# A two-layer float32 kernel: block sums stored from GpSimd's queue, one weight item prepared later, squares taken one by one

## The chip, the core and the metric

One Trainium2 chip, one of its cores. The metric is the device time of one execution in microseconds. Engines are named as in the profile: PE (TensorE, with PEld for its weight loads), DVE (VectorE), ACT (ScalarE), POOL (GpSimd), SP (SyncE). All data is float32.

## What is computed

Input x is 4 x 1024 x 32 x 32: four batches, 1024 channels, 1024 positions ("tokens"). Layer 0 is attention with 16 heads of 64, layer 1 is a bottleneck of convolutions with batch norms.

```
# layer 0, per batch, tokens x channels
q, k, v = x @ w_qkv.T + b                    # each 1024 x 1024
q, k    = rope(q), rope(k)                   # rotate even/odd pairs by cos, sin
q, k    = rmsnorm(q), rmsnorm(k)             # over all 1024 channels
ctx     = softmax(q k' / 8) v                # per head
x       = rmsnorm(ctx @ w_proj.T) * w + x
# layer 1
h = relu(bn(conv1x1(x, w1)));  h = relu(bn(conv3x3(h, w2)));  h = bn(conv1x1(h, w3))
out = relu(x + softplus(scale) * h)
```

## The kernel before

**Products.** The four projections (q, k, v and the output projection, called y) are 1024 x 1024 matrix products computed with seven block products in place of eight (Winograd's form of Strassen's scheme). That needs sums of weight blocks, called S1 to S4, and sums of blocks of x. In batch 0 the projections of q and k use one level of the scheme (`project`); each group g of weight blocks has its sums made by `operands` (L224): four loads on SP's queue (L221), four VectorE instructions (L231 to L234), and four stores of the sums to HBM, to the tensor `wd`, issued from ScalarE's queue (L239), each 256 KB. Everything else uses two levels (`project2`), and reads sums that were made ahead and stored: `wd` holds the sums of the first level, `wd2` those of the second.

**Weight items.** An item is the preparing of one outer block k (0 to 6) of one weight matrix for the second level (`prepare`, L384: four loads, VectorE L391 to L394, four stores to `wd2` from GpSimd's queue, L396), or of one block of first-level sums (`prepare_blocks`, L400: loads L405, sums L408 to L411, stores L413). In batch 0 the items of WV and the first of WQ are spread over the q, k and v projections by `weight_parts` (L1049), with their loads on GpSimd's queue, into tiles that are otherwise free (`unused`, later `rq`, the room of v, and a tile of `ts`). The other items (of WP, the rest of WQ, and WK) are made in the attention of batch 0: a list `todo` (L1127), loaded on SP's queue, and made one or two per pair of heads (L799).

**Order.** The order of TensorE, GpSimd, VectorE and ScalarE instructions is that in which the program records them. SP's queue holds the other loads. A planner spaces work: `product_done(share)` (L256) is called after each matrix product and advances a clock, 1 per product of one level and 0.5 per product of two levels; `after(n, step)` (L253) runs a step n later; `waiting` holds longer steps that run when there is room. `product_done` runs steps that are due in the order in which they were given.

**Buffers.** Weight blocks go through a ring of eight buffers of 256 KB (`chunk`, tag "w"). A load into a buffer waits for the matmuls and for the store that read the buffer before. One group of `operands` takes five of the eight, so that the last load of a group waits for the store of the first sum of the group before it.

**Rotary step.** When q (and k) of a batch are complete, `inverse_rms` (L661) sums squares by a matmul against ones (L670), and `rope` (L686) turns the eight blocks one by one: VectorE makes `qs` and `q` (L700), and GpSimd adds `qs` to `q` by two accumulating DMAs (L704). The buffers of `qs` are three, so a block waits for the additions of the third before it.

**Squares.** The sum of squares is gathered block by block. In `project2`, when a 512 x 512 block of the result is finished, `ready` (L600) plans for each of its four pieces a `done`: for k a bias on ScalarE (L608), then the square on ScalarE (L585 or L588); VectorE adds it half a unit later (L592). The pieces 0 and 1 are planned 0.5 later, the pieces 2 and 3 one unit later, beside the copies out of PSUM that ScalarE makes for TensorE (L516, L537, L542, L551, L565).

**Attention** (L744) works on pairs of heads: 16 score matmuls (L761), exponentials on ScalarE (L768), sums of the probabilities on VectorE (L772, L774), 16 matmuls with v (L780), for eight pairs and two halves of the queries. The program ends with the convolutions. A second copy of the program, with a shifted softmax, follows under a condition that is not met here.

Of the kernel before, what the change touches and what calls it, by code (L numbers as in the profile page):

```python
# [34 lines left out]
WQ, WK, WV, WP, W1 = 0, NFB, 2 * NFB, 3 * NFB, 4 * NFB  # L35
# [38 lines left out]
@with_exitstack  # L74
def layers_kernel(ctx, tc, x, wblk, w2, w3, vecs, cos, sin, out):
    nc = tc.nc
    flag = ctx.enter_context(tc.tile_pool(name="flag", bufs=1))
    bad = flag.tile([1, 1], mybir.dt.int32, name="bad")
    program(tc, x, wblk, w2, w3, vecs, cos, sin, out, bad)
    shifted = nc.values_load(bad[0:1, 0:1], min_val=0, max_val=P)  # L80
    with tc.If(shifted > 0):
        program(tc, x, wblk, w2, w3, vecs, cos, sin, out, None)
# [3 lines left out]
def program(ctx, tc, x, wblk, w2, w3, vecs, cos, sin, out, bad):  # L86


    nc = tc.nc
# [21 lines left out]
    def col(name, i=0):  # L111
        return vec[:, COL[name] + i : COL[name] + i + 1]
# [32 lines left out]
    wd = dram.tile([4 * NG, len(SUMS), P, NH * P], F32, name=f"wd{u}")  # L145
# [7 lines left out]
    with tc.tile_pool(name=f"st{u}", bufs=2) as st, ExitStack() as s:  # L153
# [48 lines left out]
        def temp(name):  # L202
            return tmp.tile([P, CH], F32, tag="tmp", name=name)
# [8 lines left out]
        def chunk(name):  # L212
            return wring.tile([P, NH, P], F32, tag="w", name=name)

        def flat(t):
            return t.rearrange("p a b -> p (a b)")

        def block(base, f, ih, name):

            t = chunk(f"w_{name}")  # L220
            nc.sync.dma_start(flat(t), wblk[base + f][:, ih * NH * P : (ih + 1) * NH * P])  # L221
            return t

        def operands(base, g, name):  # L224


            at = base // NT * NG + g
            a11, a12 = (block(base, g, ih, f"{name}_1{ih}") for ih in range(2))
            a21, a22 = (block(base, g + NG, ih, f"{name}_2{ih}") for ih in range(2))
            s1 = chunk(f"w_{name}_s1")  # L230
            nc.vector.tensor_tensor(s1, a21, a22, ALU.add)  # L231
            nc.vector.tensor_tensor(a21, a11, a21, ALU.subtract)
            nc.vector.tensor_tensor(a11, s1, a11, ALU.subtract)
            nc.vector.tensor_tensor(a12, a12, a11, ALU.subtract)  # L234
            spend(4 * TT)

            def keep():
                for o, t in enumerate((a11, s1, a21, a12)):
                    nc.scalar.dma_start(wd[at, o], flat(t))  # L239

            after(1, keep)
            return [a11, s1, a21, a12, a22]


# [2 lines left out]
        later, waiting = [], deque()  # L247
        pace = {"at": 0, "room": 0.0, "hold": False, "tables": 0.0}

        def spend(cost):  # L250
            pace["room"] -= cost

        def after(n, step):  # L253
            later.append((pace["at"] + n, step))

        def product_done(share=1.0):  # L256
            pace["at"] += share
            pace["room"] = min(pace["room"] + share, 1.2)
            due = [s for at, s in later if at <= pace["at"]]
            later[:] = [(at, s) for at, s in later if at > pace["at"]]  # L260
            for step in due:
                step()
            while waiting and pace["room"] > 0 and not pace["hold"]:
                next_waiting()

        def next_waiting():
            cost, step = waiting.popleft()
            spend(cost)
            step()

        def rest(leave=0):
            while later or len(waiting) > leave:
                product_done()
# [15 lines left out]
        def project(b, base, bs, ts, outs, bias, squares, tag, w1=None):  # L289
# [40 lines left out]
            for g in range(NG):  # L330
                c11 = outs(g)[0]
                o2 = bank("o2", f"pb_{tag}_{b}_{g}")
                product(o2, w1[NG + g], "A12", True, True)
                after(1, lambda o2=o2, c11=c11, g=g: add(c11, o2, g))
                after(2, lambda c11=c11: squares(c11, 0))
                product_done()
                if g == 1:
                    w2[0] = operands(base, 0, f"{tag}_{b}_0b")
# [45 lines left out]
        def prepare(which, base, k, alloc, queue):  # L384

            a11, a12, a21, a22 = a = alloc(f"pre_{which}_{k}")
            for i, t in enumerate(a):
                quarter(t, base, k, i // 2, i % 2, queue)

            def make():  # L390
                nc.vector.tensor_tensor(a22, a21, a22, ALU.add)  # L391
                nc.vector.tensor_tensor(a21, a11, a21, ALU.subtract)
                nc.vector.tensor_tensor(a11, a22, a11, ALU.subtract)
                nc.vector.tensor_tensor(a12, a12, a11, ALU.subtract)  # L394
                for m, t in enumerate((a11, a22, a21, a12)):
                    nc.gpsimd.dma_start(wd2[which, k, m], t)  # L396

            return make
# [174 lines left out]
        def qk_proj(b, base, bs, ts, bias, dst, tag, w1=None, two=None, bias_later=False):  # L573

            total = acc.tile([P, N], F32, tag="tot", name=f"sq{tag}_{b}")
            seen = set()

            def outs(g):
                return [dst[:, f, h] for f in (g, g + NG) for h in half]

            def squares(at, c, bias=None):
                bias = 0.0 if bias is None else bias
                if c not in seen:
                    seen.add(c)
                    nc.scalar.activation(total[:, half[c]], at, AF.Square, bias=bias)  # L585
                    return
                sq = temp(f"sq_{tag}_{b}")
                nc.scalar.activation(sq, at, AF.Square, bias=bias)  # L588

                def more():  # L590
                    spend(TT)
                    nc.vector.tensor_tensor(total[:, half[c]], total[:, half[c]], sq, ALU.add)  # L592

                after(0.5, more)

            if two is None:
                project(b, base, bs, ts, outs, bias, squares, tag, w1)
                return total

            def ready(c):  # L600
                ob, tb = (int(i) - 1 for i in c)
                for i in range(NG):
                    f = ob * NG + i

                    def done(f=f):
                        at = dst[:, f, half[tb]]
                        if bias and not bias_later:
                            nc.scalar.activation(at, at, AF.Identity, bias=col(bias, f))  # L608
                        squares(at, tb, col(bias, f) if bias and bias_later else None)

                    after(0.5 * (i // 2 + 1), done)

            project2(b, two[0], base, *two[1:], dst, False, tag, ready)
            return total

# [433 lines left out]
        def weight_parts(parts, first, step, lag, alloc):  # L1049

            for i, part in enumerate(parts):
                after(first + i * step, lambda part=part: after(lag, part(alloc, nc.gpsimd)))

        def pieces_of(tile, cols=NCH):

            at = deque(tile[:, i, h] for i in range(tile.shape[1]) for h in half[:cols])

            def alloc(name):
                at.rotate(-4)
                return [at[i] for i in range(-4, 0)]  # L1060

            return alloc


        parts_of = {
            base: [
                lambda alloc, queue, which=which, base=base, k=k: prepare(which, base, k, alloc, queue)
                for k in range(len(OUTER))
            ]
            for which, base in enumerate((WQ, WV, WP, WK))  # L1070
        }

        def blocks_of(base):
            return [lambda alloc, queue, g=g: prepare_blocks(base, g, alloc, queue) for g in range(NG)]
# [16 lines left out]
        for b in range(B):  # L1091
# [8 lines left out]
            if b == 0:  # L1100
                unused = kp.tile([P, NT, N], F32, tag="k", name="unused")
                parts = blocks_of(WV) + [parts_of[WV][k] for k in (0, 1, 6, 2)]
# [5 lines left out]
                ahead.append(two2[2][:2])  # L1108
            two = (3, *two2[1], False) if b > 0 else None
            if b == 0:  # L1110
                parts = [parts_of[WV][k] for k in (3, 4, 5)] + [parts_of[WQ][k] for k in (0, 1)]
                weight_parts(parts, 2, 4.5, 4, pieces_of(room))
            tk = qk_proj(b, WK, xs[b], ts[b], "bk", k_all, "k", None, two)
            rope(b, k_all, tk, eps_rms, 1.0 / C, (wqk_other, wqk), "k")
# [10 lines left out]
            todo = []  # L1125
            if b == 0:
                todo = blocks_of(WP) + [parts_of[WP][k] for k in (0, 1, 6, 2, 3, 4, 5)]  # L1127
                todo += [parts_of[WQ][k] for k in (3, 4, 5)] + [parts_of[WK][k] for k in (0, 1, 6, 2, 3, 4, 5)]
            made = []

            def load_parts():
# [272 lines left out]
        due = None  # L1404
        for b in range(B):
# [8 lines left out]
            for f in range(NPT):  # L1414
                for h in range(2):
# [11 lines left out]
                    due = (b, f, h)  # L1427
# [12 lines left out]
            if b == 0 and bad is not None:  # L1440
                o = ps.tile([P, CH], F32, tag="mm", name="fit")
# [127 lines left out]
```

## Time and profile before

| | before |
|---|---|
| three runs | 2689.16, 2692.98, 2693.77 us (median 2692.98) |
| profiled execution, its own time | 2691.15 us |
| its span, first to last instruction | 2689.1 us |
| PE busy | 2655.3 us, 99% |
| DVE busy | 2109.6 us, 78% |
| ACT busy | 1112.6 us, 41% |
| POOL busy | 426.8 us, 16% |
| mean granted clock of TensorE | 0.997 |
| DMA moved | 454.00 MB, mean 169 GB/s |

The stages of the profiled execution: projections of batch 0 to about 305 us, its attention to about 535 us, then the output projection and the three other batches in the same manner to about 2348 us, the first convolution to 2449 us, the second to 2569 us, the third to the end. A row of the timeline gives start, duration, engine, line, operation, output and input, how many, and in brackets how long the engine stood idle before and what ended that. Times of one execution are in microseconds from its first instruction.

### The profile page before, as it was taken

What the parts mean: (1) busy time and instruction counts of PE and PEld (TensorE: products, weight loads), DVE (VectorE), ACT (ScalarE), POOL (GpSimd) and SP (SyncE); (2) the same over time, 40 slices, a digit from 0 to 9 for tenths busy, and PEclk for the clock granted to TensorE, in tenths of its full rate; (3) what the DMA queues carried; (4) which work ended last, traced back from release to release, by engine and by line L of the source; (5) the groups of instructions that cost most, each with busy time, mean ns of one, the idle gap of its engine ahead of it and who ended that gap; (6) DMA issues with size and microseconds to landing.
All of it is one profiled execution on the core that took longest, in us unless ns stands there. A gap on an engine that the chain in (4) does not pass through costs nothing. (4 is left out here: it accounts for less than half of the span.)

```text
span 2689.1 us, 32699 instructions
## 1 busy us (share of the span) xinstructions
PE 2655.3 (99%) x11386; PEld 1650.9 (61%) x11386; DVE 2109.6 (78%) x2529; ACT 1112.6 (41%) x1551; POOL 426.8 (16%) x512
## 2 busy tenths in 40 slices
PE   8999999999999999999999999999999999999997
PEld 3448533488888333688886333888884335846843
DVE  4577899988787866788878766887878678877987
ACT  2222455533442655433343655233425554312266
POOL 2541233300001211100111211100111211010000
PEclk9999999999999999999999999999999999999999
DMA  7897767666667341457765430666784323593165
GB/s 272 301 319 210 216 213 235 229 207 219 168 179 215 62 85 35 153 150 223 189 187 150 82 56 23 207 199 180 188 230 98 62 43 99 171 286 111 63 232 207
DMA packets 259533, 454.00 MB, mean 169 GB/s; under 512 B 36320, under 2 KB 131344, under 8 KB 259360
## 3 DMA queue, kind: packets, MB, share of 16 engines
q1 hardware_dynamic: 214704, 309.09, 37.2%
q0 software_dynamic: 40048, 134.34, 19.3%
q10 hardware_dynamic: 4608, 8.39, 0.8%
q8 instruction: 93, 1.52, 0.2%
q14 instruction: 80, 0.66, 0.1%
HBM read 331.62 MB, written 97.01 MB: 159 GB/s over the span
## 5 line engine op out<-in xcount | busy, mean ns | idle before, releaser
L774 DVE TENSOR_TENSOR den<-den,p 128x1024 f32<-128x1024 f32 x384 | 470.5, 1225 | 41.0 <-DVE den L774 0.9
L768 ACT ACTIVATE p<-sc 128x1024 f32<-128x1024 f32 x512 | 476.4, 1045 | 26.4 <-PE sc L761 25.1
L761 PE MATMUL sc<-q,k 64*128 64x512 f32 x2048 | 457.9, 597 | 0.0
L761 PEld LDWEIGHTS sc<-q,k 64*128 64x128 f32 x2048 | 189.6, 186 | 266.1 <-issue 121.1
L780 PE MATMUL cx<-p,to 128*64 128x512 f32 x1536 | 340.2, 595 | 0.0
L780 PEld LDWEIGHTS cx<-p,to 128*64 128x64 f32 x1536 | 106.0, 137 | 228.2 <-issue 228.2
L742 POOL TENSOR_SCALAR q<-q,vec 128x512 f32<-128x512 f32 x64 | 125.3, 1964 | 560.5 <-DVE q L741 544.1
L457 PE MATMUL p_v<-w_v,x 128*128 128x256 f32 x928 | 210.0, 379 | 0.8 <-DVE x L428 0.7
L462 PE MATMUL p_y<-q,w_y 128*128 128x256 f32 x928 | 209.8, 379 | 0.0
L772 DVE TENSOR_TENSOR den<-p 128x1024 f32<-128x1024 f32 x64 | 78.3, 1223 | 159.9 <-ACT p L768 159.9
L462 PEld LDWEIGHTS p_y<-q,w_y 128*128 128x128 f32 x928 | 176.0, 190 | 27.1 <-issue 3.4
L457 PEld LDWEIGHTS p_v<-w_v,x 128*128 128x128 f32 x928 | 176.2, 190 | 25.9 <-DVE x L428 1.6
L785 ACT COPY q<-cx 128x512 f32<-128x512 f32 x64 | 37.5, 586 | 356.9 <-PE cx L780 356.9
L462 PE MATMUL p_k<-to,w_k 128*128 128x256 f32 x672 | 153.1, 381 | 3.2 <-ACT to L551 3.2
L462 PE MATMUL p_q<-to,w_q 128*128 128x256 f32 x672 | 152.5, 380 | 0.1
L462 PEld LDWEIGHTS p_k<-to,w_k 128*128 128x128 f32 x672 | 126.7, 190 | 24.3 <-ACT to L551 5.6
L462 PEld LDWEIGHTS p_q<-to,w_q 128*128 128x128 f32 x672 | 127.2, 190 | 19.6 <-ACT q L516 1.3
L780 PE MATMUL cx<-p,rq 128*64 128x512 f32 x512 | 113.4, 595 | 0.0
L1473 PE MATMUL c<-h,w 128*128 128x512 f32 x256 | 110.3, 592 | 0.9 <-ACT h L1375 0.9
L704 POOL DMA_DIRECT2D k<-ks x64 | 55.8, 1021 | 280.5 <-ACT p L768 96.0
L462 PE MATMUL p_y<-to,w_y 128*128 128x256 f32 x384 | 90.4, 380 | 0.9 <-DMA w_y<-wdf 0.8
L457 PE MATMUL p_v<-w_v,t 128*128 128x256 f32 x384 | 90.1, 379 | 0.7 <-DMA w_v<-wdf 0.7
(452 smaller groups left out, 4120.0 us busy)
## 6 DMA issues: line engine op xcount, KB each, us to landing
w_v<-wd2f SPq DMA_DIRECT2D x112, 256.0 KB
w_y<-wd2f SPq DMA_DIRECT2D x112, 256.0 KB
w_q<-wd2f SPq DMA_DIRECT2D x84, 256.0 KB
w_k<-wd2f SPq DMA_DIRECT2D x84, 256.0 KB
wd2f<-w_pre POOLq DMA_DIRECT2D x68, 256.0 KB, 3.9
x<-in_x_dram SPq DMA_DIRECT2D x64, 256.0 KB
q<-qs POOLq DMA_DIRECT2D x64, 256.0 KB, 5.5
k<-ks POOLq DMA_DIRECT2D x64, 256.0 KB, 4.6
```

Source lines behind the costliest of these rows:

```text
L457: nc.tensor.matmul(o[:, q].rearrange("p (g f) -> p g f", g=2), r[:, i, q * P : (q + 1) * P], wt[:, :, i, :], skip_group_check=True, **at,)
L462: nc.tensor.matmul(o[:, q], wt[:, q, i, :], r[:, i, :], skip_group_check=True, **at)
L704: nc.gpsimd.dma_start(dst[i::2, f, :], other[1 - i :: 2, :], accum_op=ALU.add)
L742: nc.gpsimd.tensor_scalar(cx, cx, col("bv", hp), None, ALU.add)
L761: nc.tensor.matmul(sc[:, j], k_all[d, hp, t * P : (t + 1) * P], q_all[d, hp, at], start=True, stop=bad is not None,)
L768: nc.scalar.activation(p, sc, AF.Exp)
L772: nc.vector.tensor_tensor(d_, probs[0], p, ALU.add)
L774: nc.vector.tensor_tensor(d_, d_, p, ALU.add)
L780: nc.tensor.matmul(o[j * HD : (j + 1) * HD, :], v[:, t, h0 : h0 + HD], probs[t][:, j], start=(t == 0), stop=(t == N // P - 1),)
L785: nc.scalar.copy(q_all[:, hp, at], o)
L1473: nc.tensor.matmul(os[i], w3t[k][f // NH][:, f % NH, :], h2[b, k][:, half[c]], start=(k == 0), stop=(k == NPT - 1),)
```

## The change

Four edits:

1. In `operands`, the four stores of the block sums are issued from GpSimd's queue instead of ScalarE's, and at once instead of one product later.
2. Steps that are due at the same time run in the order of their planned times instead of in the order given.
3. In `ready`, the four pieces of a finished block are planned at 0.5, 1.0, 1.5 and 2.0 instead of 0.5, 0.5, 1.0 and 1.0.
4. The item k = 1 of WQ is prepared in the attention of batch 0 (loads on SP's queue) instead of in the k projection of batch 0 (loads on GpSimd's queue).

```diff
             spend(4 * TT)
-
-            def keep():
-                for o, t in enumerate((a11, s1, a21, a12)):
-                    nc.scalar.dma_start(wd[at, o], flat(t))
-
-            after(1, keep)
+            for o, t in enumerate((a11, s1, a21, a12)):
+                nc.gpsimd.dma_start(wd[at, o], flat(t))
             return [a11, s1, a21, a12, a22]
...
-            due = [s for at, s in later if at <= pace["at"]]
+            due = [s for at, s in sorted(later, key=lambda e: e[0]) if at <= pace["at"]]
...
-                    after(0.5 * (i // 2 + 1), done)
+                    after(0.5 * (i + 1), done)
...
-                parts = [parts_of[WV][k] for k in (3, 4, 5)] + [parts_of[WQ][k] for k in (0, 1)]
+                parts = [parts_of[WV][k] for k in (3, 4, 5)] + [parts_of[WQ][0]]
...
-                todo += [parts_of[WQ][k] for k in (3, 4, 5)] + [parts_of[WK][k] for k in (0, 1, 6, 2, 3, 4, 5)]
+                todo += [parts_of[WQ][k] for k in (1, 3, 4, 5)] + [parts_of[WK][k] for k in (0, 1, 6, 2, 3, 4, 5)]
```

## The prediction

> **What bounds the kernel now.** I read the page's busy table first, then TensorE's list of waits, then TensorE's gaps one by one in the timeline, and last the queues that stand behind each gap.
>
> ```profile
> PE 2655.3 (99%) x11386; PEld 1650.9 (61%) x11386; DVE 2109.6 (78%) x2529; ACT 1112.6 (41%) x1551; POOL 426.8 (16%) x512
> ...
> q0 software_dynamic: 40048, 134.34, 19.3%
> q10 hardware_dynamic: 4608, 8.39, 0.8%
> ```
>
> TensorE is busy for 2655.3 of 2689.1 us. So a change that leaves its matmuls alone can win at most the 33.8 us of idle time, plus what its clock loses. Queue q10 is ScalarE's: its 8.39 MB are just the block sums that the change moves, 32 stores of 256 KB. Queue q0 is GpSimd's.
>
> ```profile
> PE pa_q L302 <- DMA x<-in_x_dram: 7.2, 2, 5.7
> PE p_k L462 <- ACT to L551: 3.2, 6, 0.8
> PE pa_k L302 <- DVE w_k_3b L233: 2.5, 1, 2.5
> ```
>
> These three waits are the ones that the change can reach: 7.2 us at the very start for x, 3.2 us in six pieces for a ScalarE copy, 2.5 us once for a block sum. Most of the rest is the 15 us after the last matmul. Windows and timeline then show what each wait really costs (a window line gives busy us of PE, PEld, DVE, ACT, POOL, then the granted clock, the DMA share and GB/s):
>
> ```profile
> 0.00:5.68 5.68, 0.00 (x1) 0.03 (x1) 0.19 (x4) 1.28 (x1) 4.61 (x12) 1.00 0.52 136
> ...
> 9.27:24.25 14.98, 14.96 (x31) 6.37 (x32) 1.55 (x9) 1.77 (x4) 0.00 (x0) 1.00 1.04 387
> ...
> 122.00:128.00 6.00, 6.00 (x16) 2.65 (x15) 4.56 (x6) 1.88 (x3) 1.03 (x2) 1.00 0.13 44
> 160.00:186.00 26.00, 26.00 (x62) 11.49 (x61) 18.56 (x24) 4.79 (x9) 15.33 (x21) 1.00 1.05 286
> ...
> 190.00:194.00 4.00, 4.00 (x7) 1.66 (x6) 2.02 (x4) 2.36 (x4) 1.45 (x3) 0.57 1.04 359
> ```
>
> The DMA engines are full from 8 us on, nearly empty at 122 to 128 us, and full at 160 to 186 us. Behind the stall at 189 us the clock is 0.57.
>
> ```profile
> 1.95 3.74 POOL L405 DMA_DIRECT2D unused<-in_wblk_dram  x7
> ...
> 182.12 0.69 DVE L391 TENSOR_TENSOR rq<-rq 128x512 f32<-128x512 f32 x1 [2.88 <-DMA rq<-in_wblk_dram]
> ...
> 187.19 0.69 DVE L231 TENSOR_TENSOR w_k_3b_s<-w_k_3b,w_k_3b 128x512 f32<-128x512 f32 x1 [2.21 <-DMA w_k_3b<-in_wblk_dram]
> ...
> 189.39 5.40 PE L302 MATMUL pa_k<-t,w_k_3b 128*128 128x512 f32 x8 [2.54 <-DVE w_k_3b L233]
> ...
> 776.88 0.57 ACT L551 COPY to<-p_k 128x512 f32<-128x512 f32 x1
> ...
> 777.50 7.17 PE L462 MATMUL p_k<-to,w_k 128*128 128x256 f32 x32 [0.81 <-ACT to L551]
> ```
>
> First row: GpSimd issues the weight loads of later work at 2 us, beside the x that TensorE waits for. Rows two to four: VectorE waits for a GpSimd load, then for w_k_3b, and TensorE behind it stands 2.54 us and then needs 5.40 us for eight matmuls that take 3.60 elsewhere. Last two: a copy queued behind squares.
>
> **What the Trainium skill says.** "TensorE: Matmul & The Clock Gate", Part 1: the array runs at half rate until it has been busy for some 3.4 us, and falls back after idleness. The trace agrees: the first matmul, at 5.68 us, starts 1 us apart from the next where later ones are 0.43 us apart, full rate comes at 12.7 us, and the clock is halved for 3.4 us after the 2.54 us stall; gaps of 1.0 us and less show no such drop. "DMA: Bandwidth & Descriptors", "Issuing engines are not separate DMA queues": DMAs of SP, ACT and GpSimd share the same 16 engines, so a move of queue saves issue time only. The trace agrees: 0 to 16 us moved 2.37 MB for SP's queue and 2.14 MB for GpSimd's together, where SP alone has 385 GB/s at 18 us. Same page, "Queues, rings and completion order": an engine takes turns between queues and works a queue in order; so a store moved into GpSimd's queue stands behind what GpSimd issued before it, and ahead of what comes after.
>
> **The change, part by part.**
>
> (1) *Stores of the block sums, ScalarE to GpSimd.* The stores now stand in program order, before GpSimd's first loads: in the built order of the changed program the four stores of w_q_0b come ahead of the first four "unused" loads, those of w_q_1b ahead of the next four. These stores wait for VectorE's L231 to L234 (38.1 us now), so the 8 x 256 KB = 2.1 MB leave the first 16 us and go to 32 to 52 us, where the DMA share is 0.43. What TensorE gains: x and w for the first matmul are 0.5 MB; I take the start at 5.0 instead of 5.68 us (3.4 if only bytes count, 0.5 MB at 385 GB/s from 2 us on, when the first packets move; 5.68 if only latency does). Eight matmuls of the first product then run without the 1.54 us wait, four at 0.85 us and four at 0.43 (half clock for 3.4 us): 5.1 us, end at 10.1 (13.65 now). The other 24 at 0.43: 10.3, so the second group starts at 20.4 instead of 24.25: **3.9 us**. What is late next: its weights and x (4 MB, which 385 GB/s brings by about 13 us) are not. VectorE's sums of x need 5.6 MB: by about 19 us instead of 26.4; from there to the end of L233 now takes 26.58 to 38.11 = 11.5 us, so 31 us; TensorE arrives at 20.4 + 13.7 = 34.1. So the 0.2 us that it waits at 38.2 goes as well: 4.1 in all. Bounds: 0 to 5.
>
> Cost on GpSimd: 32 issues of 0.54 us (row L396), 17 us beside TensorE; its queue idles 44.5 us before its first store. Cost on ScalarE: less (it stood up to 6.3 us on these), hidden either way.
>
> At 130 to 190 us it is less clear. Behind each store on GpSimd now wait the additions q<-qs of the rotary step and the loads rq<-; VectorE waits for both. The stores of w_k_2b come right behind q<-qs of block 5 and ahead of the rq loads (168 us now). The DMA engines are full there, the bytes are the same, so I expect the rq data about 1 us later (182.1 now) and the store of w_k_2b, which frees the buffer of the last w_k_3b load, about 1 us earlier than its 178.5. VectorE needs 2.9 us for L391 to L394 and 2.2 us to L233; TensorE arrives at 186.85, so the stall ends at about 188 to 189 instead of 189.39. I take **0.5 us gained**. Bounds: 4.5 gained (2.54 + 5.40 - 3.43, stall and half clock gone), 4 lost. w_k_2b had 0.7 us to spare (168.69 against 169.4), so a small stall can appear there.
>
> (2) *One weight item to the first attention.* Four loads of 256 KB leave GpSimd's queue at 182 to 188 us, which are behind the rq data that the stall waits for, so they don't help it; four stores and four sums of 0.69 (2.9 us of VectorE) leave 197 us. In attention they are added: SP loads, VectorE 2.9 us. There VectorE is busy 45.7 of 50 us, over 230 us some 20 us free; two heads' slot of 29.2 us of TensorE then holds 14 den sums of 1.225, three items of 2.9 and two products of 0.7, 27.3 us. **Zero**; without that cover at most 2.9 lost.
>
> (3) *Squares and biases one by one.* Same instructions; ScalarE's copies L516 and L551 now stand ahead of the second pair. TensorE's six waits for L551 (three of 0.81, three of 0.25, in the k stages of batches 1 to 3) have 1.3 us more each of ScalarE ahead of them than they will have, so they end: **3.2 us**. Late next: the copy L537, 3.8 us early. The sums of squares (L592) come up to two steps later, 3.4 us; the matmul that needs them comes four products after the stage, still 5 us later. Bounds: 0 to 3.2 gained, 1 lost if VectorE stands at L592. The sorting of due steps only swaps VectorE's L592 and L391 in batch 0: zero.
>
> Sum: 4.1 + 0.5 + 0 + 3.2 = 7.8 us. The profiled execution took 2691.15 us (its span 2689.1 and 2.05 around it), so 2683.4 against itself; the median of the three runs is 1.8 above it, and from that I predict **2685**.
>
> **Rivals.** *A, the sum above*: 2685. *B, the stall at 189 us goes as well*, since the store that frees the buffer lands sooner and fewer bytes follow: another 4.0, 2681. For it: the SP queue waits 8.5 us for that store. Against: VectorE waits for the rq data first. *C, the lead of the start is given back*: something bound by DMA, not by TensorE, between 60 and 200 us holds TensorE where it was; then only (3) remains, 2693 - 3.2 = 2690. For it: a DMA share of 0.98 to 1.0 at 60 to 100 us. Against: the engines empty at 122 to 128 us, so no backlog is carried past that. *D, slower*: GpSimd's queue in the k stage of batch 0. It carries 12 stores more, in order, at a time of full DMA; when q<-qs and the rq data land some 6 us later, w_k_2b stalls 5.3 us and w_k_3b 6 more than now, with 2 us of half clock for the new stall: 13.3 lost against 7.8 won, 2698.5. It outweighs the gains from about 3.5 us of delay on. Against: the bytes are those that ScalarE's queue moved in the same stretch. That the change does not do what it says can be left out: the built order shows the stores, the item and the copies where they should be, and TensorE's order unchanged.
>
> **How the numbers follow.** A 0.50, B 0.18, C 0.22, D 0.10. About 0.2% (5.4 us) is what a measurement of this kernel can tell from no change. A is beyond that in nine of ten, B always, C hardly ever: faster 0.65, same 0.26, slower 0.09. The range takes in B with a better start and C with the noise of 2 us that the three runs show: 2679 to 2691; D is left out.
>
> **What would show it.** Start: the first group (pa_q) ends near 20.4 us, no GpSimd load before about 32 us. Stall: the row for pa_k<-t,w_k_3b with 1 to 2 us of idle time and clock under 1.0. Squares: no wait of p_k for L551. Attention: no TensorE gap of more than 0.5 us in 305 to 535 us. Wrong would be made by a new wait of pa_k for w_k_2b, of p_v for w_v<-wd2f, or by a TensorE that reaches 120 us no sooner than now.

## The result and the profile after

The changed kernel takes 2683.39 us (median of six runs, 2682.62 to 2684.22) against 2692.94 us for the kernel before, in six runs beside it: a ratio of 0.9972 with a 95% interval of 0.9962 to 0.9982. It is faster by 0.28%, a little more than the 0.2% that the prediction takes as the least that can be told from no change. The profiled execution took 2684.17 us, 6.98 less than the one of before (2691.15). That one was a low run of its kernel and this one a high run, so the profiles show 2.6 us less of a difference than the medians (9.55). What follows explains the 7 us, not the rest.

First the busy table and the queues of the page of after:

```profile
PE 2651.6 (99%) x11386; PEld 1652.8 (62%) x11386; DVE 2103.8 (78%) x2529; ACT 1115.1 (42%) x1551; POOL 442.3 (16%) x540
...
q0 software_dynamic: 42288, 141.68, 20.2%
```

ScalarE's queue q10 is gone, and GpSimd's q0 carries 7.34 MB more than before: the 8.39 MB of stores, less the item's four loads. The stores went where the change sends them. Next, TensorE's list of waits (us in total, times, longest):

```profile
PE pa_q L298 <- DMA x<-in_x_dram: 5.7, 1, 5.7
PE pa_k L298 <- DVE w_k_3b L233: 1.9, 1, 1.9
PE p_y L458 <- DMA w_y<-wdf: 1.8, 1, 1.8
...
PE pa_k L298 <- DVE w_k_2b L233: 0.5, 1, 0.5
```

The wait for x came down from 7.2 in two pieces to 5.7 in one; the six waits of p_k for a ScalarE copy are gone; the wait for w_k_3b is shorter; a wait for w_k_2b is new. (From L245 on, the lines of after are those of before less 4.) The list tells nothing of what one wait costs in clock. The timeline of after (start, duration, what, and in brackets the idle time before it and what ended it) shows where these stand:

```profile
5.66 16.78 PE L298 MATMUL pa_q<-x,w_q 128*128 128x512 f32 x32 [5.66 <-DMA x<-in_x_dram]
22.27 13.90 PE L298 MATMUL pb_q<-x,w_q 128*128 128x512 f32 x32
...
34.68 2.13 POOL L401 DMA_DIRECT2D unused<-in_wblk_dram  x4
...
163.26 1.23 DVE L696 TENSOR_TENSOR qs<-q,sinT 128x1024 f32<-128x1024 f32 x1 [2.64 <-DMA q<-qs]
...
182.22 0.69 DVE L387 TENSOR_TENSOR rq<-rq 128x512 f32<-128x512 f32 x1 [5.64 <-DMA rq<-in_wblk_dram]
...
185.00 0.68 DVE L231 TENSOR_TENSOR w_k_3b_s<-w_k_3b,w_k_3b 128x512 f32<-128x512 f32 x1
...
187.19 3.70 PE L298 MATMUL pa_k<-t,w_k_3b 128*128 128x512 f32 x8 [1.91 <-DVE w_k_3b L233]
...
773.98 6.21 PE L458 MATMUL p_k<-to,w_k 128*128 128x256 f32 x28
```

Read it against the rows of before. The first matmul starts where it did (5.68 before), but the group after it starts at 22.27 instead of 24.25. GpSimd's first loads are 33 us later. At 182 us VectorE's idle time before the rq sums has doubled, and w_k_3b's own sums, which waited 2.21 us for their load before, follow now without a wait. The eight matmuls behind the stall take 3.70 us instead of 5.40. The p_k row at 773.98 begins with the matmul that waited 0.81 us before; it has no bracket, so no wait.

Both kernels execute the same 11386 matmul records in the same order. So the start of each can be subtracted from that of the same matmul before: the lead.

| where | lead of after, us |
|---|---|
| first matmul (5.66) | 0.0 |
| first matmul with w_q_0b (36.0) | 2.2 |
| w_k_2b, w_k_3b of batch 0 (168, 187) | 1.7, 2.2 |
| eight matmuls later (191) | 3.9 |
| end of the v projection (253) | 3.6 |
| end of attention of batch 0 (534) | 1.6 |
| k stages of batches 1, 2, 3 | +1.7 each |
| last matmul | 6.7 |

The gain was 2.2 at the start, 1.7 at the stall, 5.1 in the k stages; attention of batch 0 gave 2.0 back.

### The profile page after: what moved, and what is told of

The parts are those of the page before. It is cut to its first block, busy times and chain, and to the rows that moved or that the text cites. A ratio compares the mean times of both kernels' runs of the same rounds, so it can differ in the third digit from the quotient of the medians.

```text
span 2682.4 us, 32645 instructions
## 1 busy us (share of the span) xinstructions
PE 2651.6 (99%) x11386; PEld 1652.8 (62%) x11386; DVE 2103.8 (78%) x2529; ACT 1115.1 (42%) x1551; POOL 442.3 (16%) x540
```

## The experiments

Each ran beside the kernel before on the same chip. Ratios are to that, with their 95% intervals.

### One edit at a time, and all without the item

`e1_squares` is the kernel before with edits 2 and 3, `e2_stores` with edit 1, `e3_item` with edit 4; `e4_no_item` is the changed kernel without edit 4. Their diffs are the lines of the change, taken apart. Edits 2 and 3 were not tried one without the other.

e1_squares. 

> The kernel before with edits 2 and 3 alone (order of due steps, squares one by one). Theory 1, each edit brings its own gain: TensorE's waits for L551 in the k stages of batches 1 to 3 go, which by the lead of after over before at the same matmuls is 1.5 us a batch, and some 0.3 us more in each q and y stage: 4.5 to 6 us faster, start and stall at 189 us as before. Theory 2, the lead in batches 1 to 3 comes from TensorE being earlier against the other engines after edit 1: less than 2 us.

e2_stores. 

> The kernel before with edit 1 alone (stores on GpSimd's queue). Theory 1: the first group of matmuls ends some 2 us earlier, and the stall for w_k_3b gets shorter without help of the item: 2 to 4 us faster, and no gap in the attention of batch 0. Theory 2, the stall got shorter in after because the item's four loads and four stores left the DMA queue: 2 us faster only, with the stall at 2.5 us and its half clock.

e3_item. 

> The kernel before with edit 4 alone (the item k = 1 of WQ moved to the attention of batch 0). Theory 1: VectorE is late for the sums that dn reads, three or four waits of dn in the attention, 1 to 2 us slower. Theory 2: the stall at 189 us and its half clock shrink, 1 to 2 us faster in all.

e4_no_item. 

> The changed kernel without edit 4 (the item stays in the k projection). Theory 1: 1 to 2 us faster than the changed kernel, about 2682, with no wait of dn for den beyond the first pair. Theory 2: the stall of w_k_3b is back at 2.5 us or more with half clock, 2 us slower than the changed kernel, about 2685.5.

| | median, us | ratio | lead at 36, behind the stall (191), at 255, at 535 |
|---|---|---|---|
| e1_squares | 2685.28 | 0.9977 (0.9969 to 0.9985) | -0.2, 2.2, 2.3, 2.8 |
| e2_stores | 2687.47 | 0.9987 (0.9981 to 0.9994) | 2.1, 4.3, 5.3, 4.1 |
| e3_item | 2693.05 | 1.0010 (1.0002 to 1.0018) | -0.2, 2.1, 2.3, -0.8 |
| e4_no_item | 2682.07 | 0.9970 (0.9958 to 0.9982) | 3.0, 2.8, 3.7, 2.8 |
| for comparison: the change | 2683.39 | 0.9972 (0.9962 to 0.9982) | 2.2, 3.9, 3.6, 1.6 |

*Squares*: no wait of p_k for a copy, and 1.7 us gained in each k stage of batches 1 to 3, as in after. *Stores*: the gain at the start, and a changed stall, as in TensorE's waits of e2_stores:

```profile
PE p_k L458 <- ACT to L547: 3.2, 6, 0.8
...
PE pa_k L298 <- DVE w_k_3b L233: 1.0, 1, 1.0
...
PE pa_k L298 <- DVE w_k_2b L233: 0.8, 1, 0.8
```

The ScalarE waits stay, so they belong to the squares alone; the new wait for w_k_2b belongs to the stores. Of the 2.3 us that e1_squares and e3_item gain at the stall, 1.7 is clock: before has half clock behind it, they have not (the last section tells on what that hangs). *Item*: the only edit that makes the kernel slower, by 3.1 us of lead between 255 and 535 us, where e1_squares gains 0.5. The item isn't alone in losing there: the lead falls by 1.2 in e2_stores, against its theory 1, by 1.0 in e4_no_item and by 2.0 in after. So the item has about one more microsecond of the loss in after. These are single traces, and by medians e4_no_item and after can't be told apart (2682.07 and 2683.39, intervals that overlap). Edit 4 costs 0.1% alone; what it costs in the changed kernel, about 1 us, is seen in the traces only.

By medians the parts win 5.4 and 3.2 us alone and lose 2.3, 6.4 in sum; together they win 9.6, and 8.2 in e0_after below. Where the rest comes from, no run shows.

### The start

`e5_gate` leaves the stores on ScalarE, and only makes GpSimd read one column of the finished sums of w_q_0b and w_q_1b ahead of its loads:

```diff
+    gate = const.tile([P, 1], F32, name="gate")
...
             spend(4 * TT)
+
+            if at < 2:
+                nc.gpsimd.tensor_scalar(gate, a12[:, 0, 0:1], col("bq"), None, ALU.add)
 
             def keep():
```

> The kernel before, where only the first eight weight loads of GpSimd are held back until w_q_0b and w_q_1b are summed; the stores stay on ScalarE. Theory 1 (the gain of the moved stores at the start comes from the loads that no longer run beside the first x): TensorE about 2 us earlier from 24 us on, as in e2_stores, 2 us faster in the end (ratio 0.9992), and the waits of k for w_k_2b and w_k_3b as in the kernel before, since its k stage keeps its queues. Theory 2 (the gain comes from ScalarE, freed of the stores): no lead at 36 us, 0. A loss is possible if the loads then come too late for the first q blocks.

Measured: 2687.55 us, ratio 0.9985 (0.9979 to 0.9992), as much as e2_stores won. The timeline of e5_gate:

```profile
5.74 15.99 PE L306 MATMUL pa_q<-x,w_q 128*128 128x512 f32 x32 [5.74 <-DMA x<-in_x_dram]
21.56 4.03 PE L306 MATMUL pb_q<-x,w_q 128*128 128x512 f32 x9
...
32.34 0.29 POOL L239 TENSOR_SCALAR gate<-w_q_0b,vec 128x1 f32<-128x1 f32 x1 [30.39 <-DVE w_q_0b L235]
32.59 2.20 POOL L409 DMA_DIRECT2D unused<-in_wblk_dram  x4
```

The lead at 36 us is 2.9. So the start is won by the loads that stay away, and the stores only bar their way. The k stage here is that of before: a stall of 2.40 us for w_k_3b with half clock, and none for w_k_2b although TensorE comes 2.9 us earlier; so that wait isn't due to TensorE's lead, it comes with the stores in GpSimd's queue.

What may be left to win at the start is the clock. `e6_warm` puts matmuls of a constant ahead of the first product of the changed kernel, whose first accumulation overwrites them:

```diff
             for g in range(NG):
                 o = mine[g] = bank("o1", f"pa_{tag}_{b}_{g}")
+                if bad is not None and (b, tag, g) == (0, "q", 0):
+                    for _ in range(22):
+                        nc.tensor.matmul(o[:, :P], ones, ones, start=True, stop=True, skip_group_check=True)
                 product(o, w1[g], "A11", True, False)
```

> The changed kernel with 22 small matmuls of a constant ahead of the first product, whose result is overwritten: some 4.7 us of TensorE at half clock, from 1 us on, while it waits for x. Theory 1 (what is left to win at the start is the half clock, which lasts 5.65 us of busy time after the first matmul and costs half of that): pa_q runs at full clock from its start at 5.7 or shortly after, the second group starts at about 19.5 to 20.5 instead of 22.27, 2 to 2.8 us faster than the changed kernel. Theory 2 (TensorE then waits for x and w instead, which the DMA engines bring no sooner): gaps in the first group take what the clock gives, 0 to 0.5 us.

`e0_after` is the changed kernel again, on the same chip. 

> The changed kernel again, on the same chip as the three that vary it. All theories: some 9 us below the kernel before (ratio 0.9966 plus or minus 0.001). In the trace: den sums of the odd head pairs late, waits of dn at about 467, 497 and 526 us, a lead of 3.6 us at 257 us that has fallen to about 1.6 at 535; and the stall of pa_k for w_k_3b of 1 to 2.5 us, with or without half clock behind it.

Measured: e6_warm 2681.56 us, ratio 0.9960 (0.9947 to 0.9974); e0_after 2682.93 us, 0.9965 (0.9951 to 0.9979); its lead falls by 1.9 in attention, from 1.4 to -0.5, much as in after. The number of matmuls was wrong: the 22 made 44 matmul records that lasted until 8.7 us, so the first product started at 8.79, all at full clock, and the second group at 22.52: nothing was won. Half as many, in e10_best below, end as x lands.

### Attention of batch 0

Why does one item more cost time? Den sums are VectorE's sums of the probabilities; dn are the eight matmuls against ones, once per two pairs of heads, that turn them into the denominators. The end of the last den sum can be set against the start of the dn matmuls that need it (some of the eight dn wait inside their row). Time to spare, in us, in order, without the first dn of the stage, for which den is 1.1 us late in every kernel:

```
before      0.7  1.0  1.7  1.0  1.0  0.6  0.4
e1_squares  1.0  1.0  1.7  1.3  1.3  1.0  0.8
e2_stores   1.0  0.9  1.7  1.0  0.6  0.1 -0.6
e4_no_item  0.6  0.8  1.4  0.9  0.9  0.8 -0.4
e6_warm     1.0  0.3  0.4  0.3  0.3  0.5  0.3
e0_after    1.0  1.0  1.0  0.5  0.0 -0.7 -0.8
after       1.0  1.0  1.0  0.2 -0.6 -0.2 -0.8
e3_item     1.0  1.0  1.0 -0.1  0.0 -1.1 -1.3
```

With 21 items (the first four) the den sums are late in the last pair at most; with 22 (the others) they have little to spare or are late in two to four places. How late differs from run to run: e6_warm has all 22 and just keeps up. The first suspicion was the place of the double slots. A slot is one pair of heads for one half of the queries. 22 items in 15 slots put two into each even slot but the first, just ahead of the den sums of the odd pair; `e7_odd_slots` puts them into the odd slots:

```diff
-                for _ in range(len(extra) - -(-steps_in_all * max(slots - 1 - c * NHP - hp, 0) // slots)):
+                i = c * NHP + hp + 1
+                keep = -(-steps_in_all * max(slots - i, 0) // slots)
+                if steps_in_all == 22:
+                    keep = max(22 - i - i // 2, 0)
+                for _ in range(len(extra) - keep):
```

> The changed kernel, where the 22 pieces of weight work of the first attention are given out so that the slots with two of them are the odd ones instead of the even ones. Theory 1 (the moved item costs 1.7 to 2.7 us because its double slots fall just ahead of the den sums that the dn matmuls need): no dn waits at 467, 497 and 526, the lead of 3.6 us at 257 us is still there at 535, some 1.5 to 2 us faster than the changed kernel. Theory 2 (VectorE is simply too full with one item more): the dn waits go to other places and the sum stays within 0.5 us.

Measured: 2684.21 us, 0.9972 (0.9960 to 0.9983), no better. The den sums are late from the second of these places on (0.1, -1.3, -0.7, -0.1, -0.7, 0.0, 0.0), and the lead falls from 2.3 at 257 us to -1.0. The theory of the even slots fell.

The timeline of after shows what stands in the way, here from one dn row to the next, 29 us later. An item is loaded into w_pre (L378), summed (L387 to L390) and stored (L392):

```profile
437.58 1.07 PE L803 MATMUL dn<-den,ones 128*32 128x512 f32 x8
...
438.71 0.59 ACT L819 COPY rec<-dn 128x512 f32<-128x512 f32 x1 [0.43 <-PE dn L803]
...
442.30 2.20 POOL L392 DMA_DIRECT2D wd2f<-w_pre  x4
...
444.70 0.37 SPq L378 DMA_DIRECT2D w_pre<-in_wblk_dram  x1
445.17 0.50 SPq L820 DMA_DIRECT2D densf<-rec  x1
445.77 4.11 SPq L378 DMA_DIRECT2D w_pre<-in_wblk_dram  x3
449.98 0.42 SPq L823 DMA_DIRECT2D few<-densf  x1
452.45 0.25 DVE L826 RECIPROCAL few<-few 128x16 f32<-128x16 f32 x1 [1.32 <-DMA few<-densf]
452.62 0.63 DVE L387 TENSOR_TENSOR w_pre<-w_pre,w_pre 128x512 f32<-128x512 f32 x1
...
466.74 1.68 PE L803 MATMUL dn<-den,ones 128*32 128x512 f32 x8
```

The denominators are copied from dn to rec at 438.7 and travel through HBM into the tile few, by two transfers on SP's queue (densf is the tensor in HBM). But an item's load stands ahead of each, waiting for its buffer, which is free when GpSimd's stores of the item before have landed. So rec, ready at 439.3, leaves at 445.17; few leaves at 449.98; VectorE stands 1.32 us for it, and behind it in VectorE's order are two items and seven den sums. The dn row at 466.74 takes 1.68 us instead of 1.07. SP's own waits in attention say the same (after, 340 to 535 us; us in total, times, longest):

```profile
SPq L378 <- DMA wd2f<-w_pre: 67.9, 31, 9.2
```

The kernel before has nearly the same (69.5 us), and VectorE stands for few as long in both (340 to 535 us; before, then after):

```profile
DVE few L830 <- DMA few<-densf: 4.2, 5, 1.4
...
DVE few L826 <- DMA few<-densf: 4.2, 4, 1.3
```

So these waits did not come with the change. With one item fewer, the den sums of before still keep 0.4 us or more; the item's own sums use that up.

`e8_loads` sends the items' loads through GpSimd's queue, behind the stores that they wait for anyway:

```diff
-                    made.append(todo.pop(0)(pieces, nc.sync))
+                    made.append(todo.pop(0)(pieces, nc.gpsimd))
```

> The changed kernel, where the pieces of weight work of the first attention are loaded by GpSimd's queue instead of SP's. Theory 1 (the moved item costs TensorE 1.7 to 2.7 us in attention because its loads stand, waiting for their buffers, ahead of the two transfers densf<-rec and few<-densf in SP's queue; the reciprocal of few then comes late, and VectorE's weight sums and den sums behind it): few arrives some 5 us earlier in each pair, den is done 0.5 us or more before dn in every pair, the lead over the kernel before is kept from 257 to 535 us, some 2 us faster than the changed kernel, 2681. Theory 2 (VectorE itself is full): the dn waits stay, within 0.5 us of the changed kernel.

The same pair in the timeline of e8_loads:

```profile
438.38 0.59 ACT L819 COPY rec<-dn 128x512 f32<-128x512 f32 x1 [0.43 <-PE dn L803]
439.00 0.50 SPq L820 DMA_DIRECT2D densf<-rec  x1
...
440.68 0.33 SPq L823 DMA_DIRECT2D few<-densf  x1
...
443.77 0.72 POOL L378 DMA_DIRECT2D w_pre<-in_wblk_dram  x1 [0.41 <-DMA wd2f<-w_pre]
...
450.52 0.25 DVE L826 RECIPROCAL few<-few 128x16 f32<-128x16 f32 x1
```

Few leaves 9 us sooner and VectorE no longer stands for it. With all 22 items the den sums have 1.0 us to spare in every place of the table, no wait of VectorE for few is left, and the lead grows from 3.9 at 257 us to 4.6 at 535. VectorE is busy 213.8 us from 305 to 535 us, more than in after (210.7). So VectorE was not too full; SP's queue held it up. Since e8_loads moves the loads of all 22 items, it does not tell what the loads of the one moved item do there. By time alone (2681.99 us, ratio 0.9965, 0.9951 to 0.9978) e8_loads can't be told from the changed kernel.

### The stall at 187 us, and all together

`e9_lag` makes each item of the k stage one product later, so that on VectorE it follows the block sums of w_k_2b and w_k_3b:

```diff
-                weight_parts(parts, 2, 4.5, 4, pieces_of(room))
+                weight_parts(parts, 2, 4.5, 5, pieces_of(room))
```

> The changed kernel, where the sums of each weight item of the k stage of batch 0 are made one product later, so that on VectorE they stand behind the block sums of w_k_2b and w_k_3b instead of ahead. Theory 1 (the stall of 1.9 to 2.2 us at 187 us is VectorE standing for the rq data ahead of w_k_3b's sums): the stall falls to under 0.5 us and no half clock follows, some 2 to 4 us faster than the changed kernel before attention. Theory 2 (w_k_3b's own load is nearly as late): a stall of 1 to 2 us stays, now ended by that load.

Timeline of e9_lag:

```profile
167.43 3.70 PE L298 MATMUL pa_k<-t,w_k_2b 128*128 128x512 f32 x8 [0.97 <-DVE w_k_2b L233]
...
184.70 3.60 PE L298 MATMUL pa_k<-t,w_k_3b 128*128 128x512 f32 x8
```

w_k_3b's sums start at 181.06 instead of 185.00, the stall is gone, and the lead behind it is 6.5 instead of 3.9. The wait for w_k_2b grew to 0.97, and attention took 2.5 us back by late den sums (five of seven late, by up to 1.2 us): this kernel keeps the items' loads on SP's queue. Time: 2683.00 us, 0.9970 (0.9957 to 0.9982), no better than after.

`e10_best` has both edits, and 11 small matmuls in place of 22. 

> The changed kernel with both edits above and with 11 small matmuls of a constant ahead of the first product (some 4.7 us at half clock, from 1 us on, to end as x lands). If each theory holds: second group at about 20 instead of 22.27, no stall at 187 us, no dn waits; 2 + 3 + 2 us less than the changed kernel, 2676. If the starts are bound by x and not by the clock, and VectorE is full: 2680 to 2683.

The start of TensorE in the timeline of e10_best:

```profile
1.05 4.98 PE L325 MATMUL pa_q<-ones 128*128 128x128 f32 x22 [1.05 <-DVE eps_bn L106]
5.90 13.97 PE L298 MATMUL pa_q<-x,w_q 128*128 128x512 f32 x32
19.71 1.45 PE L298 MATMUL pb_q<-x,w_q 128*128 128x512 f32 x3
```

Full clock comes at 5.82 us, the 32 matmuls take 13.97 us instead of 16.78, and the second group starts 2.6 us before that of after. The lead is 4.8 at 36 us, 7.9 behind the w_k_3b matmuls, 8.4 at 535 us, 15.0 at the last matmul. As in e8_loads, the den sums have 1.0 us to spare in every place of the table. Time: 2675.59 us (2675.08 to 2676.51), where 2676 was expected; ratio 0.9939 (0.9926 to 0.9953). That is below the interval of after (0.9962 to 0.9982) and just touches that of e0_after (0.9951 to 0.9979), which ran on another chip; on its own chip its slowest execution is below the fastest of e8_loads (2679.13) and e9_lag (2681.21).

## Why the prediction was right, and where it was not

The forecast of 2685 (2679 to 2691, faster 0.65) held: 2683.39. Rival A was the one that came, but its terms were not the right size, and errors on both sides met: that the sum came so close is luck in part.

**Start, 4.1 predicted, 2.2 measured.** The loads left as foreseen (none before 34.68 us), and the wait of 1.54 us inside the first product went. Two terms were mis-sized. The first matmul was to start at 5.0; it starts at 5.66, and between 5.5 and 6.1 in all kernels whose TensorE has nothing else to do before, with or without GpSimd's loads: the bound of 5.68 came true. What sets it, no run shows, but it isn't GpSimd's loads. And half clock was put at 3.4 us after the first matmul; it lasted 5.65 (5.66 to 11.31). "TensorE: Matmul & The Clock Gate", Part 1, of the Trainium skill says that the window is "free-running", which the prediction passed over: half clock ends with a window, and not a fixed 3.4 us after the first matmul. The runs agree: in the eight kernels that start without a gap and without matmuls of a constant, it lasted from 2.83 us (6.06 to 8.89, e8_loads, where the window in which work began was enough) to 5.65 (after, where a whole window followed on the rest of the first); in those with a gap at the start up to 9.23 (5.56 to 14.79, e1_squares).

**Stall, 0.5 predicted, 1.7 measured.** That the rq loads would stand behind the stores of w_k_2b was right (issued from 171.86 us, 168.08 before), and so was that w_k_3b's load would cease to be last. The rq data, forecast 1 us later, came at the same time as before (182.22 and 182.12), and e9_lag shows that without the rq sums ahead of w_k_3b's there is no stall.

The sum has an error here. It took TensorE's arrival at the stall from before (186.85), as if there were no lead, and added 0.5 to the 4.1 of the start. By its own end of the stall, 188 to 189 us against 189.39, all but 0.4 to 1.4 us of that lead would have gone into a longer stall, as rival C has it. The lead outlived the stall because it ended sooner than forecast, at 187.19: 2.2 us before its old end, as much as the lead.

The size missed the clock too. The prediction kept about 3.4 us of half clock behind the shortened stall; in after there was none, in e0_after, with 2.10 us of stall, there was, and its lead behind the stall is 2.0 where after has 3.9. So the 1.7 us of this term (half of 3.4) is luck of the run. The new wait for w_k_2b was foreseen as possible; it is 0.45 us, 0.8 in e2_stores.

**Item, zero predicted, about 1 us lost in after and 3 alone** (attention loses 2.0 in after, 1.0 without the item in e4_no_item; 3.1 in e3_item, and 0.1 in e6_warm, which has the item). This step failed: the cover. The count of VectorE's work held (27.3 of 29.2 us per two slots, some 20 us free; from 305 to 535 us VectorE was busy 210.3 of 230 us before). But free time isn't cover where VectorE can't use it. Behind the loads on SP's queue that wait for their buffers stand densf and few, and VectorE stood 4.2 us for few with seven den sums behind it. The prediction put the item's loads on that queue ("In attention they are added: SP loads") and asked neither what they wait for there nor what stands behind them. In e8_loads, without these waits, the same 22 items cost TensorE nothing in this stretch. The loss it allowed for without cover (2.9) was of the right size.

**Squares, 3.2 predicted, 5.1 measured**, beyond its upper bound of 3.2. The six waits end. In each k stage the lead grows by 1.7 us, 0.6 more than the waits shown (0.81 and 0.25). Half of that is how idle time is shown: a matmul's end is modelled 0.16 us past the start of the next (a row of eight lasts 3.60 us, the next starts after 3.43), so each idle time shown is short by that. The rest came in steps of 0.1 us, whose cause no run shows. The q stages of batches 1 to 3, which the prediction left out, gained 0.3 us each, in e1_squares too.

Sum: 2.2 + 1.7 + 5.1 and 2.0 lost in attention, 7.0, and 0.3 lost net of small gains, such as those of the q stages, and losses such as the longer wait of p_y for w_y<-wdf at 2276 us (1.78, 0.48 before), which wasn't tried. Against the prediction's 7.8 that is close because the lost 1.9 of the start and the 2.0 of attention are met by 1.2 and 1.9 on the other side. C fell, since the lead reached 253 us; D too, since GpSimd's queue cost 0.45 us at w_k_2b while the other stall became shorter. B came only in e9_lag, by another cause than the one it named.

Of the tests named in advance, one was nearly blind: "no TensorE gap of more than 0.5 us in 305 to 535 us". The one gap above 0.5 in after is 0.86 us at 534.06, where p_y waits for the last rec (0.53 before), while 2 us were lost in this stretch. Eight dn matmuls waited one by one, and their row only grew, from 1.07 to 1.68, 1.33 and 1.87 in the three late places. Another test, clock under 1.0 behind the stall, failed in after and held in e0_after.

## What to carry to other kernels

When a step is moved into a stage, price each of its DMAs by the queue that it joins: what does a load wait for there, and which short transfer that an engine needs stands behind it. A lead and the end of a later stall don't add up: where the stall ends at a fixed time, it swallows the lead. A move that wins by keeping other transfers away (the stores as a gate) can be had alone, with one small instruction. Compare two traces by the lead at the same matmul, stage by stage: it finds losses that no list of waits shows.

## What was not expected of the hardware

The clock changes of all thirteen traces lie on a grid of 3.413 us that runs through the whole execution: in those with a drop behind the stall, it comes 52.0 or 53.0 steps after the first full clock. What decides over the drop is how busy TensorE is within one window of that grid, so the place of a stall counts as well as its length. Two kernels with the same stall of 2.20 us for w_k_3b, in windows of that grid (us, busy time of PE, PEld, DVE, ACT, POOL, then clock, DMA share, GB/s); first e4_no_item:

```profile
183.80:187.21 3.41, 1.21 (x4) 0.37 (x3) 3.30 (x6) 1.32 (x2) 1.45 (x2) 1.00 1.04 323
187.21:190.62 3.41, 3.41 (x6) 1.35 (x5) 3.22 (x6) 1.26 (x2) 1.67 (x3) 0.50 1.05 390
```

Then e8_loads:

```profile
182.97:186.38 3.41, 1.65 (x4) 0.38 (x2) 3.27 (x6) 1.32 (x2) 1.62 (x3) 1.00 1.03 260
186.38:189.79 3.41, 2.97 (x7) 1.44 (x8) 3.38 (x6) 1.26 (x2) 1.83 (x4) 1.00 1.04 398
```

In e4_no_item, one window holds the whole stall, TensorE is busy in 1.21 of 3.41 us, and the next window runs at half clock. In e8_loads a boundary cuts the stall, the emptier window has 1.65 us of work, and the clock stays. Length counts too: after, with 1.91 us of stall, and e0_after, with 2.10, lie on the same grid to 0.06 us.

```profile
185.39:188.80 3.41, 1.61 (x4) 0.87 (x5) 3.31 (x6) 1.55 (x3) 1.43 (x3) 1.00 1.02 339
...
185.33:188.74 3.41, 1.37 (x3) 0.68 (x4) 3.31 (x6) 1.36 (x3) 1.70 (x5) 1.00 1.01 335
```

Behind the first the clock stayed, behind the second it was halved. Over all windows of the thirteen traces that ran at full clock, one busy to 40% or less was followed by half clock, one busy to 47% or more was not; where between them it turns, no run shows. The way up asked for more: a window at half clock, busy to 79% (e1_squares, 7.97 to 11.38 us), was followed by another at half clock, one busy to 83% (e8_loads, 5.48 to 8.89 us) by full clock. "After idleness", as the prediction put it after the page of the Trainium skill that it names, is too coarse: in these traces a window that is partly busy is enough. A stall of 2.0 us so costs 2.0 or 3.7 us by chance.
